# Another order of turns, key products, normalizations and layer borders in a two-layer attention kernel

## The chip, the cores and the metric

The kernel runs on one core of one Trainium2 chip. The metric is device time in microseconds (us) of one execution. All arithmetic is in 32-bit floating point.

## The reference

There are 8 sequences (batches) of 512 tokens with 512 features. A graph layer is followed by a self-attention layer with 16 heads. Cut to what matters:

```python
# layer 0: graph attention; every token attends to the first 20 tokens, in two directions d
self_feat = concat(x, cond) @ W_self.T + b_self
for d in range(2):
    aff = (self_feat @ Wq[d].T + bq[d]) . (self_feat[:, :20] @ Wk[d].T + bk[d])      # per head
    w = softmax(where(edges > 0, aff, NEG) + edge_bias)
    output += einsum(w, self_feat[:, :20]) @ Wout[d] + bout[d]
x = x + relu(output)
# layer 1: self-attention with conditional layer norm
h = gamma(cond) * layernorm(x) + beta(cond)
q, k, v = h @ Wqkv.T + bqkv
out = (softmax(q @ k.T) / sqrt(512)) @ v @ Wp.T + bp          # 16 heads of 32
h1 = out + x
return gamma * layernorm(h1) + beta + h1
```

## The kernel before, in words

Four engines compute: TensorE (PE) multiplies and transposes, VectorE (DVE), ScalarE (ACT) and GpSimd (POOL) do the rest; SyncE (SP) issues most transfers. Every engine works through its own queue in the order in which the program writes its instructions (`manual_schedule`), so the order of the lines in a step is the order on each engine. A tile pool with n buffers gives out its buffers in turn, and the next user waits until the last one's readers are through.

**Layer 0** walks 32 slots, one for each batch and each block of 128 tokens. For slot n it transposes the weights of slot n (`turn_weights`, tile `ptw`), normalizes those of slot n+1 (`normalize0`: exponential on ACT, sum and reciprocal on DVE, multiplication on POOL), and makes the scores of slot n+2 (`scores0`: `pss` on PE, an addition on DVE, then on POOL the mask L480 and the edge terms L481; `less_top`: maximum on DVE, subtraction on POOL). `result0` makes the slot's result (`po`), which DVE adds to x and SP writes to `mid`. In the last slots PE gets products of layer 1 for batch 0 between them: `q_or_k` and `value` (`pqk`, `pv`).

**Layer 1** walks 128 steps: 7 batches of 16 steps (4 head groups g times 4 token blocks c), and a last batch of 16 steps with the token blocks outermost. `at` is the step's number in its batch, 0 to 15. In step n:

- `scores(n+1)` (PE, tile `s`), `tops(n+1)` (DVE, two maxima over 1024 elements), `exps(n+1)` (ACT, four exponentials), `normalize(n+1)` (DVE `reciprocal` of `den`, then POOL multiplies each of four tiles `e`), in two pairs of heads;
- `turn_probs(n, j)`: PE transposes one of four `e` tiles into a PSUM bank `pt`, and ACT or DVE copies it to `et`;
- in even steps `weigh(n-2)` and `weigh(n-1)` (PE, tile `pao`), in the last batch one `weigh` in every step;
- two job slots (`job(b, 2*at)` and `job(b, 2*at+1)`), one ahead of the transposes of j = 2 and one ahead of those of j = 3. The list `JOBS[b]` fills them: products for the next batch's queries, keys and values (`product`, tile `pst`; seven products each, by a Strassen scheme whose sums of token quarters `token_sums` and of weights `weight_sums` are made ahead), or the output projection of the batch before (`project`, `ppj`). `None` is a hole. A product's bank is emptied by DVE (L715, L722, L724), a projection's too (L737).
- `turn(b+1, f)`: PE transposes 128 features of the next batch's normalized tokens Z into a bank `pz`, and ACT (L127) or DVE (L129) writes the gated result to HT. `norm_stats` and `norm` make Z.
- `finish(b, c, part)` for finished blocks: "statistics" on DVE and POOL, "norm" on DVE (L749, L750), "sums" on POOL (L753, L754) with the transfer to `out`. The table `FINISH` says in which step.

The banks `pt`, `pst`, `ppj`, `pz` come from one ring of three (`ps_g`), `pao` from a ring of one (`ps_a`): a transpose or product waits until the bank three users back has been emptied.

Of the kernel before, what the change touches and what calls it, by code (L numbers as in the profile page):

```python
# [19 lines left out]
P = 128  # L20
# [24 lines left out]
def graph_then_self_attention(ctx: ExitStack, tc: tile.TileContext, x, x_t, near, near_t, labels, w_self_t, wq, wk_t,  # L45
# [68 lines left out]

        nc.gpsimd.tensor_tensor(XQ[b][:, c, :], XQ[b][:, c, :], bp_bc, ALU.add)

    def turn(b, f, by_scalar=True):

        if f == 0:
            pool = turned if b == 1 else feat  # L120
            HT[b] = pool.tile([P, C, N], F32, tag="turned" if b == 1 else "feat", name=f"ht_{b}")
        pz = bank(f"pz_{b}_{f}")
        for c in range(C):
            nc.tensor.transpose(pz[:, c * P:(c + 1) * P], Z[b][:, c, f * P:(f + 1) * P], ident)  # L124
        factor, term = (gates_t[:, i, f, b:b + 1] for i in range(2))
        if by_scalar:
            nc.scalar.activation(HT[b][:, f, :], pz, AF.Identity, bias=term, scale=factor)  # L127
        else:
            nc.vector.tensor_scalar(HT[b][:, f, :], pz, factor, term, ALU.mult, ALU.add)  # L129

    class Group:

# [38 lines left out]
    with ExitStack() as l0:  # L171
# [295 lines left out]
        def scores0(b, c):  # L467
            cut = slice(c * P, (c + 1) * P)
            pss = pair(f"pss_{b}_{c}")
            for i in range(2):  # L470
                on = slice(i * HM // 2, (i + 1) * HM // 2)
                o = pss[:, i, :HM // 2]
                for k in range(C):
                    nc.tensor.matmul(o, SF[b][:, k, cut], KQ[b][:, k, on], start=(k == 0), stop=(k == C - 1))  # L474
            t = three.tile([P, H, D2], F32, tag="t", name=f"t_{b}_{c}")
            nh = H // 2
            for i in range(2):
                nc.vector.tensor_tensor(t[:, i * nh:(i + 1) * nh], pss[:, i, :HM // 2].rearrange("p (h e) -> p h e", h=nh),
                                        QR[b][:, i * HM // 2:(i + 1) * HM // 2].rearrange("p (h e) -> p h e", h=nh), ALU.add)
            nc.gpsimd.tensor_tensor(t, t, MASK[b][:, c, None].to_broadcast([P, H, D2]), ALU.mult)  # L480
            nc.gpsimd.tensor_tensor(t, t, ADD[b][:, c, None].to_broadcast([P, H, D2]), ALU.add)  # L481
            T[b, c] = t

        def less_top(b, c):
            t = T[b, c]
# [65 lines left out]

        slots = [(b, c) for b in range(B) for c in range(C)]
        scores0(*slots[0])
        less_top(*slots[0])
        scores0(*slots[1])
        normalize0(*slots[0])
        less_top(*slots[1])
        for c in (0, 1):
# [3 lines left out]
        load_vt(2)  # L562
        for n, (b, c) in enumerate(slots):
            turn_weights(b, c)
            if n + 1 < len(slots):
                normalize0(*slots[n + 1])
            if n + 2 < len(slots):
                scores0(*slots[n + 2])
            if b + 1 + c // 2 < B:
                self_feat(b + 1 + c // 2, ((c + 2) % 4,))  # L570
            if 26 <= n < len(slots) - 2:
# [7 lines left out]
            if n in (24, 25):  # L579
                for f in (2 * (n - 24), 2 * (n - 24) + 1):  # L580
                    turn(0, f)
            for i in {26: (0,), 27: (1,), 29: (2,), 30: (3,)}.get(n, ()):
                group = q_or_k(i, 0) if i < 2 else value(i - 2)
                group.half(0)
                group.half(1)
            if n == 10:
                gate_columns(gb)
            result0(b, c)
            if n < 26:
                less_top(*slots[n + 2])  # L590
            if b + 1 + c // 2 < B:
# [29 lines left out]
                norm_stats(0, n - 15, early)  # L621
            for i in {22: (0, 1), 23: (2, 3)}.get(n, ()):
                norm(0, i, early)
            if n == 30:
                for i in range(C):
                    norm_stats(1, i)
            if n == 31:
                for i in range(C):
                    norm(1, i)

# [176 lines left out]
    def normalize(n, pair):  # L809
        at = slice(2 * pair, 2 * pair + 2)  # L810
        nc.vector.reciprocal(DEN[n][:, at], DEN[n][:, at])  # L811
        for j in (2 * pair, 2 * pair + 1):
            nc.gpsimd.tensor_scalar(E[n][j], E[n][j], DEN[n][:, j:j + 1], att_scale, ALU.mult, ALU.mult)  # L813

    def turn_probs(n, j, copy):
        pt = bank(f"pt1_{n}_{j}")
# [5 lines left out]
    def weigh(n):  # L822
        b, g, c = steps[n]
        last = b == B - 1
        if c == 0 or last:
            PAO[b, g] = ps_a.tile([P, 512], F32, tag="pao", name=f"pao_{b}_{g}_{c}")
        at = slice(c * P, (c + 1) * P)
        for k in range(C):
            for j in range(4):
                h = 4 * g + j  # L830
                nc.tensor.matmul(PAO[b, g][DH * j:DH * (j + 1), at], V[b][:, k, DH * h:DH * (h + 1)],  # L831
                                 ET[n, j][:, k, :], start=(k == 0), stop=(k == C - 1))
# [19 lines left out]
    def made(i, *ns):  # L852
        return [("product", i, n) for n in ns]

    def out_of(*cs):
        return [("project", c, n) for c in cs for n in range(2)]

    q, k, v = 0, 1, 2
    keys_and_queries = (made(q, 1, 2, 6, 5) + made(k, 1, 2, 6) + made(q, 3) + made(k, 5, 3)
                        + made(q, 4, 7) + made(k, 4, 7))  # L860
    JOBS = {0: [("own", i, f, n) for i, f in ((k, 1), (q, 2), (k, 2), (q, 3), (k, 3)) for n in range(2)]
            + made(v, 1, 2, 6, 5, 3, 7, 4) + [None] + keys_and_queries}
    for b in range(1, B - 1):
        pp = out_of(0, 1, 2, 3)
        JOBS[b] = [("turn", 1), ("turn", 2)] + pp + made(v, 1, 2, 6, 5, 3, 7, 4) + [None] + keys_and_queries

    JOBS[B - 2][4:17] = [pp[2], None] + pp[3:] + made(v, 1, 2) + [None] + made(v, 6, 5, 3)
    LAST = made(v, 4, 7) + [("project", B - 2, 0, 0), None]
    for job in ((B - 2, 0, 1), (B - 2, 1, 0), (B - 2, 1, 1), (B - 2, 2, 0), (B - 2, 2, 1), (B - 1, 0, 0), (B - 1, 0, 1), (B - 2, 3, 0),
                (B - 1, 1, 0), (B - 1, 1, 1), (B - 2, 3, 1), (B - 1, 2, 0), (B - 1, 2, 1)):  # L870
        LAST += [("project",) + job, None]
    JOBS[B - 1] = LAST

    FINISH = {}
    for b in range(1, B):
        for block, first, second in (((b - 1, 0), 2, 4), ((b - 1, 1), 4, 6), ((b - 1, 2), 6, 8), ((b - 1, 3), 7, 9)) if b < B - 1 else (
                ((b - 1, 0), 2, 3), ((b - 1, 1), 4, 5), ((b - 1, 2), 6, 7), ((b, 0), 8, 9), ((b, 1), 11, 12), ((b - 1, 3), 12, 13),
                ((b, 2), 14, 15)):
            FINISH.setdefault((b, first), []).append(block + ("statistics",))
            for part in ("norm", "sums"):  # L880
                FINISH.setdefault((b, second), []).append(block + (part,))
    OWN = {}

    def finish_parts(part):
# [4 lines left out]
    def job(b, slot):  # L889
# [4 lines left out]
        if kind == "own":  # L894
            i, f, n = of
            if n == 0:
                OWN[0] = q_or_k(i, f)
            OWN[0].half(n)
        elif kind == "turn":
            turn(b + 1, of[0], by_scalar=False)  # L900
        elif kind == "product":
            product(b + 1 if b < B - 1 else b, *of)
        else:
            project(*(of if b == B - 1 else [b - 1] + of))

    with tc.manual_schedule():
# [5 lines left out]
        scores(0)  # L912
        for pair in range(2):
            tops(0, pair)
        for pair in range(2):
            exps(0, pair)
        for group in (value(2), value(3)):
            group.half(0)
            group.half(1)
        for pair in range(2):  # L920
            normalize(0, pair)
        group = q_or_k(0, 1)
# [3 lines left out]
        for n, (b, g, c) in enumerate(steps):  # L926
# [3 lines left out]
            if more:  # L930
                scores(n + 1)
                for pair in range(2):
                    tops(n + 1, pair)
            if b == 0 and at < 4:
                turn(1, at)
            elif at < 2 and not last:
                turn(b + 1, 3 * at)
            if last and at > 0:
                if at > 1:
                    weigh(n - 2)  # L940
# [6 lines left out]
            if b + 2 < B:  # L947
                for i in range(2) if at == 12 else ():
                    norm_stats(b + 2, i)
                for i in range(C) if at == 14 else ():  # L950
                    norm(b + 2, i)
            early = n % 2 == 0 or last
            if more and early:
                exps(n + 1, 0)
            turn_probs(n, 0, nc.scalar.copy)
            if more and last:
                exps(n + 1, 1)
            turn_probs(n, 1, nc.vector.tensor_copy if last else nc.scalar.copy)
            if more and not early:
                exps(n + 1, 0)  # L960
            if more and not last:
                exps(n + 1, 1)
            if n > 0 and n % 4 == 0 and (not last or at == 0):
                outputs(n - 1)
            job(b, 2 * at)
            if more:
                normalize(n + 1, 0)
            if last:
                finish_parts("norm")
            finish_parts("statistics")  # L970
            if at in (12, 13) and b + 2 < B:
                norm_stats(b + 2, at - 10)
            if b == 0 and at < 12:
                weight_sums((v, q, k)[at // 4], at % 4)
            turn_probs(n, 2, nc.vector.tensor_copy if 0 < b < B - 1 and at < 2 else nc.scalar.copy)
            job(b, 2 * at + 1)
            if more:
                normalize(n + 1, 1)
            turn_probs(n, 3, nc.vector.tensor_copy)

            finish_parts("sums")
            sums = at - (4 if b == 0 else 1)
            if 0 <= sums < 3 and b + 1 < B:
                for i in {0: (0,), 1: (1, 2), 2: (3,)}[sums]:
                    token_sums(b + 1, i)
            if at == 9 and b > 0 and b + 2 < B:
                fetch(b + 2)
            for i, when in enumerate(range(C) if last else (10, 11, 12, 15)):
                if at == when:
# [61 lines left out]
```

## Time and profile before

| | us |
|---|---|
| median of 3 runs | 1345.51 (1344.25 to 1348.13) |
| the profiled execution | 1345.76 |
| its span, first to last instruction | 1344.0 |
| PE busy | 1314.8 (98%) |
| DVE busy | 957.6 (71%) |
| POOL busy | 757.6 (56%) |
| ACT busy | 668.1 (50%) |

The profiled execution is 0.25 us above the median, and 1.76 us of it lie outside its span. Durations come from that one execution. Matmul rows overlap: a row starts while the one before it still drains, so that a step of PE is measured from the start of one `s` row to the start of the next.

### The profile page before, as it was taken

The page shows a single profiled execution, that of the slowest core. Times are in us where ns is not written, and L with a number is a line of the kernel's source. Part 1 is how long each engine was busy: PE and PEld are TensorE (multiplying, and loading weights), DVE is VectorE, ACT ScalarE, POOL GpSimd, SP SyncE. Part 2 cuts the span into 40 slices and gives each one's busy share as a digit, 9 for nine tenths or more (in the row PEclk, how much of TensorE's full clock was granted, in tenths as well). Part 3 has the DMA queues.
Part 4 walks back from the last instruction along what each step waited for, and adds up shares of the span by engine and source line. Part 5 has one row for each costly group of instructions (what it writes and reads, how often), then busy time and mean ns, then how long its engine had stood idle before and what let it go on. Part 6 is the DMA issues. An engine that isn't in the chain of part 4 may idle for free.

```text
span 1344.0 us, 29289 instructions
## 1 busy us (share of the span) xinstructions
PE 1314.8 (98%) x11251; PEld 969.2 (72%) x11251; DVE 957.6 (71%) x1746; ACT 668.1 (50%) x1639; POOL 757.6 (56%) x867
## 2 busy tenths in 40 slices
PE   9999999999999999999999999999999999999997
PEld 6566666666664677777777777777777777777775
DVE  4567777677644578677767868777786877776886
ACT  1322223222225656665656566565665656665664
POOL 0255654555652455566466556646655664764776
PEclk9999999999999999999999999999999999999999
DMA  9624452252221000001002000100200010010010
GB/s 333 199 85 143 146 189 88 94 182 100 90 79 55 2 2 1 2 17 64 2 9 71 2 2 17 64 2 10 71 2 1 25 57 1 17 33 1 10 41 32
DMA packets 46521, 78.63 MB, mean 59 GB/s; under 512 B 9872, under 2 KB 14416, under 8 KB 46384
## 3 DMA queue, kind: packets, MB, share of 16 engines
q1 hardware_dynamic: 45440, 75.57, 16.5%
q8 instruction: 90, 1.47, 0.4%
q0 software_dynamic: 512, 0.66, 0.2%
q10 hardware_dynamic: 432, 0.55, 0.1%
q14 instruction: 47, 0.39, 0.1%
HBM read 59.27 MB, written 17.49 MB: 57 GB/s over the span
## 4 chain that ended last, share of the span: by engine, by line
PE 87%; DVE 8%; POOL 2%; DMA 1%; issue 1%; ACT 1%; POOLq 0%; SPq 0%; DVEq 0%; ACTq 0%
PE pst L700 17%; PE pt L818 17%; PE s L794 10%; PE pao L831 9%; PE pss L474 8%; PE ppj L735 7%; PE psf L303 6%; PE pqk L141 2%; PE po L515 2%; DVE top L801 1%; PE pz L124 1%; DVE o L750 1%; PE pw L443 1%; PE ptw L503 1%; PE pq L424 1%
## 5 line engine op out<-in xcount | busy, mean ns | idle before, releaser
L813 POOL TENSOR_SCALAR e<-e,den 128x512 f32<-128x512 f32 x512 | 362.7, 708 | 356.6 <-DVE den L811 256.5
L806 ACT ACTIVATE e<-s,top 128x512 f32<-128x512 f32 x512 | 349.2, 700 | 169.2 <-DVE top L801 169.2
L801 DVE TENSOR_REDUCE top<-s 128x2 f32<-128x1024 f32 x256 | 301.1, 1217 | 27.1 <-PE s L794 26.5
L818 PEld LDWEIGHTS pt<-ident,e 128*128 128x128 f32 x2048 | 234.1, 141 | 95.2 <-issue 41.7
L818 PE MATMUL pt<-ident,e 128*128 128x128 f32 x2048 | 290.9, 276 | 10.6 <-DVE den L811 6.2
L820 ACT COPY et<-pt 128x512 f32<-128x512 f32 x356 | 200.1, 596 | 133.4 <-PE pt L818 132.3
L794 PE MATMUL s<-k_pair,q_pair 32*128 32x512 f32 x992 | 144.9, 640 | 0.0
L474 PE MATMUL pss<-kq,sf 128*128 128x320 f32 x512 | 143.2, 433 | 1.0 <-DVE kq L431 1.0
L831 PEld LDWEIGHTS pao<-et,v 128*32 128x32 f32 x4096 | 107.4, 110 | 49.3 <-issue 48.5
L831 PE MATMUL pao<-et,v 128*32 128x128 f32 x4096 | 126.7, 274 | 0.5 <-ACT ao L847 0.5
L474 PEld LDWEIGHTS pss<-kq,sf 128*128 128x128 f32 x512 | 94.9, 190 | 37.5 <-ACT sf L310 1.5
L735 PE MATMUL ppj<-w,ao 128*128 128x256 f32 x496 | 117.9, 381 | 0.0
L303 PE MATMUL psf<-vt,ws 128*128 128x512 f32 x256 | 115.0, 592 | 0.0
L806 ACT ACTIVATION_READ_ACCUMULATOR e<-s,top 128x1 f32 x512 | 110.0, 215 | 0.0
L820 DVE COPY et<-pt 128x512 f32<-128x512 f32 x156 | 105.4, 675 | 2.5 <-PE pt L818 2.4
L735 PEld LDWEIGHTS ppj<-w,ao 128*128 128x128 f32 x496 | 89.4, 190 | 11.0 <-ACT ht L127 1.4
L497 POOL TENSOR_TENSOR t<-t,den 128x640 f32<-128x640 f32 x32 | 40.8, 1274 | 83.5 <-DVE den L496 82.9
L303 PEld LDWEIGHTS psf<-vt,ws 128*128 128x128 f32 x256 | 48.3, 190 | 50.7 <-issue 46.6
L505 ACT COPY wt<-ptw 128x640 f32<-128x640 f32 x32 | 22.2, 693 | 106.8 <-PE ptw L503 106.4
L737 DVE TENSOR_TENSOR xq<-ppj,xq 128x256 f32<-128x256 f32 x62 | 26.3, 424 | 61.1 <-PE ppj L735 61.1
L492 ACT ACTIVATE t<-t 128x640 f32<-128x640 f32 x32 | 23.6, 737 | 80.1 <-POOL t L489 80.1
L489 POOL TENSOR_TENSOR t<-t,top 128x640 f32<-128x640 f32 x32 | 40.7, 1273 | 37.4 <-DVE top L488 37.4
(236 smaller groups left out, 1935.5 us busy)
## 6 DMA issues: line engine op xcount, KB each, us to landing
x<-in_x SPq DMA_DIRECT2D x8, 1024.0 KB
mid<-x SPq DMA_DIRECT2D x32, 256.0 KB
xq<-mid SPq DMA_DIRECT2D x8, 1024.0 KB
out<-o SPq DMA_DIRECT2D x31, 256.0 KB
vt<-in_x_t SPq DMA_DIRECT2D x7, 1024.0 KB
labels<-in_labels SPq DMA_DIRECT2D x16, 440.0 KB
wq<-in_wq SPq DMA_DIRECT2D x4, 1024.0 KB
gate<-gates SPq DMA_DIRECT2D x8, 512.0 KB
```

Of the source, the lines that this page charges most:

```text
L303: nc.tensor.matmul(psf[f], ws[:, k, f * P:(f + 1) * P], VT[b][:, k, :], start=(k == 0), stop=(k == C - 1))
L474: nc.tensor.matmul(o, SF[b][:, k, cut], KQ[b][:, k, on], start=(k == 0), stop=(k == C - 1))
L497: nc.gpsimd.tensor_tensor(tv, tv, den.to_broadcast([P, 2 * H, NG]), ALU.mult)
L700: nc.tensor.matmul(out[:, m, :], fixed[:, k, m * P:(m + 1) * P], moving[:, k, :], start=(k == 0), stop=(k == 1))
L735: nc.tensor.matmul(out, AO[b, k][:, c * P:(c + 1) * P], wp[:, k, on], start=(k == 0), stop=(k == C - 1))
L794: nc.tensor.matmul(S[n][j // 2][:, j % 2, :], Q[b, g][on, c * P:(c + 1) * P], K[b, g][on, :], start=True, stop=True)
L801: nc.vector.tensor_reduce(TOP[n][:, 2 * pair:2 * pair + 2], S[n][pair], AX.X, ALU.max, negate=True)
L806: nc.scalar.activation(e, S[n][pair][:, j % 2, :], AF.Exp, bias=TOP[n][:, j:j + 1], accum_out=DEN[n][:, j:j + 1])
L813: nc.gpsimd.tensor_scalar(E[n][j], E[n][j], DEN[n][:, j:j + 1], att_scale, ALU.mult, ALU.mult)
L818: nc.tensor.transpose(pt[:, k * P:(k + 1) * P], E[n][j][:, k * P:(k + 1) * P], ident)
L820: copy(et, pt.rearrange("p (k n) -> p k n", k=C))
L831: nc.tensor.matmul(PAO[b, g][DH * j:DH * (j + 1), at], V[b][:, k, DH * h:DH * (h + 1)], ET[n, j][:, k, :], start=(k == 0), stop=(k == C - 1))
```

## The change

It alters only orders, places and engines; every matmul of before is there after. In six parts:

1. **Turns.** `turn(b+1, f)` runs at the head of steps 1 to 4, one block of features in each, always with ACT. Before, blocks 0 and 3 were at the head of steps 0 and 1 and blocks 1 and 2 in the job slots of step 0, the latter two with DVE (for batch 1: all four at the heads of steps 0 to 3).
2. **Keys.** Key products 4 and 7 of a batch move from its predecessor's step 15 to its own step 0 ("late"). In the last batch it is the value products 4 and 7, in slots 0 and 2 (before: 0 and 1).
3. **Holes.** The two slots that this frees become holes in the second slots of steps 10 and 12, beside the one in step 8; the order of the query and key products changes with it.
4. **Finishing.** In batches 1 to 6 the "norm" parts stand in steps 4, 6, 6, 8 (before: 4, 6, 8, 9), the statistics in steps 2 to 5 (before: 2, 4, 6, 7). `token_sums` follow the turns by a step or so. The third block's copy in steps 0 and 1 goes from DVE to ACT. The next-but-one batch is fetched a step earlier.
5. **Between the layers.** In slot 29 the last slot's scores are summed on DVE ahead of slot 30's denominators, and its edge terms are added by DVE (`add_edges`) and not by POOL. `value(1)` and `value(2)` are put around the last two slots' transposes and results. Batch 1's `norm_stats` and `norm` move from layer 0's last slots behind layer 1's first `tops` and into its step 0.
6. **The end.** In the last batch the blocks are finished in order (6,0) to (6,3), (7,0) to (7,2), always at an odd step; step 1 takes the order of copies and exponentials that odd steps have in other batches; the last `weigh` gets a bank of the ring of three; the last step's `e` for j = 3 is scaled by DVE, and its second reciprocals stand behind the copy.

```diff
@@ layer 0
+        def add_edges(b, c, engine=nc.gpsimd):
+            engine.tensor_tensor(T[b, c], T[b, c], ADD[b][:, c, None].to_broadcast([P, H, D2]), ALU.add)
...
+            if n + 3 == len(slots):
+                scores0(*slots[n + 2])
             if n + 1 < len(slots):
                 normalize0(*slots[n + 1])
+            if n + 3 < len(slots):
+                scores0(*slots[n + 2])
             if n + 2 < len(slots):
-                scores0(*slots[n + 2])
+                add_edges(*slots[n + 2], nc.vector if n + 3 == len(slots) else nc.gpsimd)
...
-            for i in {26: (0,), 27: (1,), 29: (2,), 30: (3,)}.get(n, ()):
-                group = q_or_k(i, 0) if i < 2 else value(i - 2)
+            group = {26: lambda: q_or_k(0, 0), 27: lambda: q_or_k(1, 0), 29: lambda: value(0), 30: lambda: value(1),
+                     31: lambda: value(2)}.get(n, lambda: None)()
+            if group:
                 group.half(0)
-                group.half(1)
+                if n < 30:
+                    group.half(1)
...
             result0(b, c)
+            if n >= 30:
+                group.half(1)
@@ layer 1
-            nc.gpsimd.tensor_scalar(E[n][j], E[n][j], DEN[n][:, j:j + 1], att_scale, ALU.mult, ALU.mult)
+            engine = nc.vector if n + 1 == len(steps) and j == 3 else nc.gpsimd
+            engine.tensor_scalar(E[n][j], E[n][j], DEN[n][:, j:j + 1], att_scale, ALU.mult, ALU.mult)
...
-        if c == 0 or last:
+        if n + 1 == len(steps):
+            PAO[b, g] = bank(f"pao_{b}_{g}_{c}")
+        elif c == 0 or last:
...
+    late = [("late", k, n) for n in (4, 7)]
+    JOBS = {b: (late + out_of(0, 1, 2, 3) if b else own) + made(v, 1, 2, 6, 5, 3, 7, 4) + [None]
+            + made(q, 1, 2) + made(k, 1) + [None] + made(q, 6, 5) + made(k, 2) + [None] + made(k, 6) + made(q, 3) + made(k, 5, 3)
+            + made(q, 4, 7) + [None] for b in range(B - 1)}
+    JOBS[B - 2][14:] = (made(v, 3) + made(q, 1, 2) + [None] + made(q, 6, 5) + made(k, 1) + [None] + made(k, 2, 6) + made(q, 3) + [None]
+                        + made(k, 5, 3) + made(q, 4, 7) + made(k, 4, 7))
+    JOBS[B - 1] = [("late", v, 4), None, ("late", v, 7)]
...
-        for block, first, second in (((b - 1, 0), 2, 4), ((b - 1, 1), 4, 6), ((b - 1, 2), 6, 8), ((b - 1, 3), 7, 9)) if b < B - 1 else (
-                ((b - 1, 0), 2, 3), ((b - 1, 1), 4, 5), ((b - 1, 2), 6, 7), ((b, 0), 8, 9), ((b, 1), 11, 12), ((b - 1, 3), 12, 13),
+        for block, first, second in (((b - 1, 0), 2, 4), ((b - 1, 1), 3, 6), ((b - 1, 2), 4, 6), ((b - 1, 3), 5, 8)) if b < B - 1 else (
+                ((b - 1, 0), 2, 3), ((b - 1, 1), 4, 5), ((b - 1, 2), 6, 7), ((b - 1, 3), 8, 9), ((b, 0), 10, 11), ((b, 1), 12, 13),
                 ((b, 2), 14, 15)):
...
-        for group in (value(2), value(3)):
-            group.half(0)
-            group.half(1)
+            if pair == 0:
+                group = value(3)
+                group.half(0)
+                group.half(1)
...
-            if b == 0 and at < 4:
-                turn(1, at)
-            elif at < 2 and not last:
-                turn(b + 1, 3 * at)
+            if n == 0:
+                for i in range(C):
+                    norm(1, i)
+            if 0 < at <= C and not last:
+                turn(b + 1, at - 1)
...
-            early = n % 2 == 0 or last
+            each = last and at != 1
+            early = n % 2 == 0 or each
```

## The prediction

> **What bounds the kernel now.** I read the page first, then the chain at the border of the layers, then the rows of each engine in order of time. On the page:
>
> ```profile
> PE 1314.8 (98%) x11251; PEld 969.2 (72%) x11251; DVE 957.6 (71%) x1746; ACT 668.1 (50%) x1639; POOL 757.6 (56%) x867
> PE 87%; DVE 8%; POOL 2%; DMA 1%; issue 1%; ACT 1%; POOLq 0%; SPq 0%; DVEq 0%; ACTq 0%
> ```
>
> PE is the bound, and the change leaves its work alone. It can only win back what PE loses in small waits, 13% of the chain at most. There are three places. The first is the border of the layers, in the chain in order of time (start, us, what):
>
> ```profile
> 391.74 1.55 POOL t L480
> ...
> 393.36 1.55 POOL t L481
> ...
> 399.26 1.28 POOL t L497
> ...
> 400.58 0.78 PE ptw L503 x5
> ...
> 404.74 1.22 DVE top L801
> ...
> 406.77 8.80 PE pv L141 x16
> ```
>
> From 391.7 to 400.6 one slot's mask, edges, maximum, subtraction, exponential, sum and scaling run in a row while PE ends its other work at 398.7; from 404.6 to 406.8 PE waits for DVE to empty a bank. And 16 `pv` matmuls take 8.80 us where 16 at the usual 0.43 take 6.9. The stretches say why (PE, PEld, DVE, ACT, POOL busy, then PE's granted clock):
>
> ```profile
> 407.00:411.00 4.00, 4.00 (x6) 1.58 (x6) 2.65 (x6) 1.83 (x6) 1.15 (x2) 0.57 0.27 96
> 411.00:415.00 4.00, 4.00 (x11) 1.73 (x10) 0.17 (x1) 0.65 (x2) 1.64 (x3) 1.00 0.92 363
> ```
>
> The clock was halved behind the idle time: the wait costs twice, first as itself and then as five `pv` at 0.85 in place of 0.43.
>
> The second place is step 9 of every batch, here batch 2. DVE's rows, then PE's:
>
> ```profile
> 598.28 0.54 DVE L749 TENSOR_SCALAR o<-xq,mv_h 128x512 f32<-128x512 f32 x1
> 598.85 0.69 DVE L750 TENSOR_TENSOR o<-o,gate 128x512 f32<-128x512 f32 x1
> ...
> 604.51 1.33 DVE L749 TENSOR_SCALAR o<-xq,mv_h 128x512 f32<-128x512 f32 x1
> 605.87 1.65 DVE L750 TENSOR_TENSOR o<-o,gate 128x512 f32<-128x512 f32 x1
> 607.44 0.68 DVE L715 TENSOR_TENSOR q_pair<-pst,vec 128x512 f32<-128x512 f32 x1
> ```
>
> ```profile
> 601.06 1.21 PE L794 MATMUL s<-k_pair,q_pair 32*128 32x512 f32 x8
> ...
> 605.34 1.89 PE L700 MATMUL pst<-ht,w 128*128 128x256 f32 x8
> 608.27 0.63 PE L818 MATMUL pt<-ident,e 128*128 128x128 f32 x4 [1.03 <-DVE den L811]
> 608.82 1.14 PE L794 MATMUL s<-k_pair,q_pair 32*128 32x512 f32 x8
> ```
>
> A step of PE is 1.07 for `s`, 1.02 for the first two `pt` (0.44 each and 0.15 for the switch), 1.73 for each product, 0.44 for each later `pt`: 6.43 odd, 8.31 even with `pao` (1.88). Step 9 lasts 608.82 - 601.06 = 7.76, so 1.33 are lost: DVE's norm takes 2.98 instead of 1.23 beside POOL's sums, the bank of the product is emptied at 608.12, and the last `pt` needs that bank.
>
> The third is the last batch, where a wait of ACT's copies holds PE:
>
> ```profile
> PE pt L818 <- ACT et L820: 2.9, 5, 1.1
> ```
>
> **The change part by part.** (a) *Border, part 5.* PE's own work from the last `pss` (ends 388.17) to `s_1` is four `pv` (4 x 3.43), `pqk` 3.43, three `po` (1.55), two `ptw` (0.55), `s` 1.07 = 24.0 with switches 24.2, so `s_1` could start at 412.3; it starts at 418.94. 6.6 are lost. After: DVE adds at 388.4 (before at 390.28, behind `den`), mask 389.3 to 390.9. The edge terms go to DVE: no such row; the nearest is L750 with two SBUF inputs, 0.69 for 512 elements; L495's sum over 640 takes 0.82, which I take. It meets POOL's L497 (1.27), now behind the mask. The row: L750 takes 1.65 for its 0.69 beside POOL's L754, and 1.06 beside POOL's scalings L813, at 1259.1. [...] Free of it the addition ends at 391.8[...]. The rest of the chain is as before, 5.6 (394.93 to 400.53): `t` is ready at 397.4 or 398.6. PE, with half of `value(1)` and `value(2)` on either side, reaches that `ptw` at 398.7; cost nothing either way, 0.1 to 1.3 of margin. `po_7_3`, the rest of `value(2)`, `s_0` at 404.3 follow with no wait; DVE empties the last `po` at 403.4, and `pv` 3 needs only ACT's copy, 405.1. Four statistics (3.95 in a row before) now stand on DVE behind both maxima and ahead of the reciprocals, with POOL's four powers (0.55) ahead of `e_0`: first `e_0` at 413.4, PE wants it at 413.3; `pt` loses 0.2 to 0.4. The norms (1.91) behind `tops(1)` delay `e_1` to 418.7, wanted at 420. Gain 6.3, bounds 3 and 6.8.
>
> (b) *Turns and keys, parts 1 and 2.* Before: steps 0 and 1 of batch 2 last 543.01 - 536.39 = 6.62 and 550.27 - 543.01 = 7.26; their content is 6.31 and 6.87; 0.7 are lost, 0.26 of it as the projection at 545.74 waits for ACT to empty the `pz` bank (ring of three). After, steps 1 and 3 have that same order (`s`, `pz`, two `pt`, projection): 2 x 0.26. In even steps `pao` covers ACT's 0.78, but `pz` behind `s` and `pao` behind `pz` pay the 0.15 switch once more (net one more per batch). Paid: 0.7. So nothing is won. ACT has 4.3 in a step with three copies of 0.53, and 5.1 with a turn, of 6.9: hidden; DVE is freed of 1.6. Late k4 and k7 put 2.0 of L724 into step 0, an 8.3 step in which DVE has 3.3 else: hidden; keys of pair 1 are used in step 7. Behind the late v7 waits step 114's `pao`, 3 us later.
>
> (c) *Finishing, part 4.* The norm leaves step 9: 1.33 back in batches 1 to 6. Two norms in step 6: DVE before had `tops` to 583.2, one norm to 584.5 and then 1.11 of waiting for the product at 585.4. A second norm (1.26) ends at 585.7: 0.2 late, and the bank is due at 587.4. But POOL, with t2 and t3 in step 4 (1.28 each), runs about 2.3 late into step 6, and its t4 (two inputs) meets a norm. [...] By the rows 0.37 + 0.9, PE loses 0 to 0.5; I take 0.3. POOL's four sums there (5.2) leave e_40 0.35 of margin. Fetch on SP: one step earlier and still behind the same `out` issue, read four steps later; nothing. In the last batch the gate's transfer falls behind one `out` issue, two steps ahead of its use as before; nothing.
>
> (d) *Holes, part 3.* PE only gives the 1.73 to step 0. The hole of step 8 ran without loss (`e_41` at 601.15, `pt` at 602.20). In step 12 DVE has `tops` 2.36, three statistics 3.0, k2 0.87, reciprocals 0.3, copy 0.67 = 7.2 for 6.58 of PE: reciprocal at 6.6 into the step, second scaled `e` at 8.4, wanted at 8.3. 0.2 lost, 0 to 0.6. Batch 0 has weight sums before its holes; there one `pt` lost 0.35 in step 9, and it will again after step 10: 0.4 more.
>
> Batches 1 to 5: 2.03 won, 0.7 + 0.3 + 0.2 paid = 0.8 each, 4.1. Batch 6, without statistics: 1.1. Batch 0: -0.4. Middle: 4.8.
>
> (e) *The end, part 6.* Step 1 lasts 1247.12 - 1241.22 = 5.90 with content 4.69: `pt` waits for ACT's copy behind two exponentials. With odd order and the moved v7 this goes: 1.2. Step 12 lasts 1320.61 - 1313.38 = 7.23, as norm and statistics share it; the steps after a norm alone last 6.22, the others 5.8 to 5.95. After: 0.8 won. From 1326.91 to 1334.04 PE does 4.9 of work in 7.13: POOL brings `e` 2 and 3 of the last step at 1329.9 and 1330.8, and `pao` waits 0.49 for the ring of one. POOL without a sum in step 12 is 0.5 earlier, one `e` (0.7 to 0.8) is DVE's (by L749, 0.54, up to 1.06), the bank wait goes: 1.6. DVE's last norm then stands behind the last copy, idle until the last projection. End: 3.6, bounds 1.5 and 5.
>
> Sum: 6.3 + 4.8 + 3.6 = 14.7, all inside the span; what lies around it, and the 6.3 us from the last matmul to the end, stay. 1345.76 - 14.7 = 1331.1, less 0.25, by which the profiled execution stands above the median: **1330.8**. [...]
>
> **The rivals.** *The border pays half* (15%): POOL's place in the queue, or the bank for `pv` 3, holds PE another 3 us[...]. For: several semaphores gate it and the margins are 0.1 to 0.3. Against: PE has products to run. 1335.5. *The stall only moves* (17%): step 6 or 12 loses another 1.0 in six batches, for which the 1.33 of step 9 speaks; against, POOL stood idle for 4.6 at that norm. 1336.8. *Slower* (4%): the doubled norm in step 6 collides in full, 2 x 2.98. DVE then has 10.7 for 8.31 of PE (2.4 lost), POOL's sums start late and hold `e_40` (1.3), and steps 8 and 12 lag 1.0: 5.4 a batch instead of 1.2, 6 x 4.2 = 25: 1356. It decides from 4.4 a batch on; POOL's other rows in step 6 are scalings, which cost 0.37. *Nothing arrives* (4%): half of border and end and no middle, 1341 to 1346. *Better* (8%): step 6 and 12 lose nothing and border and end come in full: 1326.
>
> **How the numbers follow.** The main case (52%) spans 1328 to 1334. A measurement of this kernel tells 0.3% or 4 us from no change. 8 in 10 reach from 1326.5 over border and moved stall to 1338. Faster by more than 4 us (below 1341.5) are the main case, better, the half border and the moved stall but for 1% of its tail: 0.91; same are that 1% and "nothing arrives": 0.05; slower 0.04.
>
> **What would show it.** Right: `ptw` without a wait for POOL near 398.7, no half clock at the border, `s_1` near 412.5; step 9 at 6.43; projections of steps 1 and 3 still 0.26 late; the last batch's step 1 near 6.5 without a wait for `et`. Wrong: a wait of `pt` in steps 6, 7 or 12 above 0.6, L749 and L750 of step 6 above 2 us together per block, or a batch period (116.64 now) that falls by less than 0.4 or by over 1.5.

## The result

| | us |
|---|---|
| before, median of 4 runs | 1344.88 (1344.19 to 1348.13) |
| changed, median of 4 runs | 1335.14 (1334.97 to 1335.69) |
| ratio, 95% interval | 0.9924 (0.9906 to 0.9941) |
| the changed kernel's profiled execution, its span | 1335.18, 1333.4 |

The changed kernel is faster by 9.7 us. Forecast were 14.7, from 1345.51 to 1330.8, in a range of 1326.5 to 1338.0: the sign and the range held, and a third of the gain did not come.

The page of the changed kernel, the rows that answer to those of before (engines, then the chain that ended last):

```profile
PE 1314.7 (99%) x11251; PEld 967.4 (73%) x11251; DVE 943.7 (71%) x1723; ACT 683.2 (51%) x1664; POOL 755.6 (57%) x865
PE 86%; DVE 8%; POOL 2%; issue 2%; DMA 1%; ACT 1%; POOLq 0%; SPq 0%; DVEq 0%; ACTq 0%
```

PE's busy time is the same to 0.1 us, but that is the sum of two opposite changes: between the last `pss` and the end of `s_1` it falls from 27.5 to 25.3, and in each of batches 1 to 5 it rises by 0.37. The chain's shares hardly move; they do not tell where time was won. What tells is the length of each step, from the end of its `s` row to the end of the next. Worked out from PE's rows, batch 2 (counted from 0, as everywhere below):

```
step             0    1    2    3    4    5    6    7    8    9   10   11   12   13   14   15 | batch
before        6.75 7.12 8.31 6.43 8.31 6.42 8.31 6.43 6.64 7.70 8.31 6.43 8.31 6.43 8.31 6.43 | 116.64
changed       8.31 7.13 8.89 7.12 8.90 6.43 8.53 6.43 6.64 6.48 6.58 6.54 6.58 6.73 8.52 6.43 | 116.23
recip_first   8.31 7.13 8.90 7.12 8.90 6.43 8.53 6.43 6.64 6.43 6.58 6.43 6.58 6.43 8.52 6.43 | 115.76
keys_first    8.31 7.13 8.90 7.12 8.90 6.43 8.53 6.43 6.64 6.47 6.58 6.53 6.58 6.73 8.31 6.43 | 116.01
old_middle    6.75 7.12 8.31 6.43 8.31 6.43 8.31 6.43 6.65 6.47 8.31 6.43 8.31 6.43 8.31 6.43 | 115.41
orders_odd    8.31 6.99 8.90 6.99 8.90 6.43 8.31 6.43 6.64 6.43 6.58 6.43 6.58 6.43 8.31 6.43 | 115.06
```

(The rows below the second are experiments.) Steps 10 and 12 are shorter by the 1.73 of the product that left them. Step 9 won 1.22. But steps 6, 11, 13 and 14 each became longer with no work added.

The fronts of two executions differ (the last `pss` ended at 388.33 before and at 388.73 after), so the sum is made from there to the last matmul: 949.43 before, 938.42 after, 11.0 won. By parts, with the two products (3.46) that move from batch 0 to batch 6 set against each other: border to `s_1` +6.48, batch 0 -1.56, batches 1 to 5 +0.41 each, batch 6 +0.55, the last batch +3.49. These are profiled executions: the one of before stands 0.88 above the median of the table, and the front of the changed one is 0.40 longer, so that 11.0 here are 9.7 there.

**The border.** The chain in order of time (start, us, what), then a stretch of the windows view (PE, PEld, DVE, ACT, POOL busy, PE's granted clock, DMA share, GB/s):

```profile
399.25 0.55 PE ptw L503 x5
399.80 1.72 PE pv L138 x4
...
404.79 1.07 PE s L799 x8
405.86 3.63 PE pv L138 x8
409.49 3.43 PE pqk L138 x8
412.93 1.08 PE s L799 x8
```

```profile
407.00:411.00 4.00, 4.00 (x10) 1.71 (x9) 3.83 (x10) 2.86 (x8) 1.11 (x2) 1.00 0.99 346
```

The chain goes through PE alone where it went through POOL, DVE and ACT; eight `pv` take 3.63 where 16 took 8.80 (0.45 for 0.55 each); the clock is 1.00 where it was 0.57. Of the 6.48, 4.26 are PE's idle time, which is gone, and 2.21 are busy time; some 1.7 of the latter (an estimate) are the half of the 3.41 us that the granted clock stood at 0.50 (shown below).

**The end.** PE's waits for ACT's copies were 2.9 us in five, all in the last batch. The waits for POOL's `e`, there too, were these (what waits, for what, us in total, times, longest):

```profile
PE pt L818 <- POOL e L813: 1.1, 2, 0.8
```

In the changed kernel the same two waits are

```profile
PE pt L824 <- ACT et L826: 1.6, 6, 0.4
PE pt L824 <- POOL e L819: 0.8, 1, 0.8
```

One of the six, 0.37, is in step 0 of batch 0, so 1.2 are left in the last batch. The second line, at 1319.7, is the tail's wait for one `e`: it became shorter and did not go.

### The profile page after: what moved, and what is told of

The parts are those of the page before. It is cut to its first block, busy times and chain, and to the rows that moved or that the text cites. A ratio compares the mean times of both kernels' runs of the same rounds, so it can differ in the third digit from the quotient of the medians.

```text
span 1333.4 us, 29328 instructions
## 1 busy us (share of the span) xinstructions
PE 1314.7 (99%) x11251; PEld 967.4 (73%) x11251; DVE 943.7 (71%) x1723; ACT 683.2 (51%) x1664; POOL 755.6 (57%) x865
## 4 chain that ended last, share of the span: by engine, by line
PE 86%; DVE 8%; POOL 2%; issue 2%; DMA 1%; ACT 1%; POOLq 0%; SPq 0%; DVEq 0%; ACTq 0%
PE pst L705 18%; PE pt L824 16%; PE s L799 9%; PE pss L471 9%; PE pao L839 8%; PE ppj L740 8%; PE psf L300 6%; PE po L515 2%; PE pqk L138 2%; DVE top L806 2%; PE pz L124 1%; PE ptw L503 1%; PE pw L440 1%; PE pq L421 1%; PE pv L138 1%
## 5 line engine op out<-in xcount | busy, mean ns | idle before, releaser
L826 ACT COPY et<-pt 128x512 f32<-128x512 f32 x369 | 208.8, 595 | 105.1 <-PE pt L824 103.9
L826 DVE COPY et<-pt 128x512 f32<-128x512 f32 x143 | 96.7, 677 | 3.1 <-PE pt L824 2.8
L126 ACT ACTIVATE ht<-pz,gates_t 128x512 f32<-128x512 f32 x32 | 24.7, 778 | 74.2 <-PE pz L124 74.2
```

Of the source, the lines that this page charges most:

```text
L826: copy(et, pt.rearrange("p (k n) -> p k n", k=C))
```

## The experiments

Each is the changed kernel with one edit. Times are medians.

### border_back and edges_pool: the border

```diff
# border_back: part 5 undone
# edges_pool
-                add_edges(*slots[n + 2], nc.vector if n + 3 == len(slots) else nc.gpsimd)
+                add_edges(*slots[n + 2])
```

> The changed kernel with part 5 undone (the border between the layers as before, batch 1's statistics and norms back in the last slots). Theory: in the changed kernel s_1 comes 6.08 us sooner, but 0.58 of that is given back in step 0, where PE waits for e_0, e_1 and a copy. So undone it is 1335.1 + 5.5 = 1340.6 us (1339.5 to 1341.6), with the idle DVE, the wait of ptw for POOL and pv at half clock back. Rival: the give-back in batch 0 (1.56 in all) belongs to the border's statistics and norms: then only +4.5, 1339.6, and the waits of steps 11, 13, 14 of batch 0 are gone. Rival: step 0 loses the same either way: +6.1, 1341.2.

> The changed kernel; only the last slot's edge terms are added by POOL as in the other slots. DVE's addition took 1.88 us in the changed kernel (391.37 to 393.25), beside POOL's L497 (391.30 to 392.57); alone some 0.82 was estimated. POOL's additions take 1.53, and this one would stand behind L497: from 392.6 to 394.1, 0.9 later, so that the last scaling ends at 399.8, and PE reaches ptw at 399.25: some 0.5 lost, 1335.6 us (1335.2 to 1336). Rival: PE has other work behind it and nothing is lost: 1335.1. Rival: the short wait makes more of itself (clock, bank of pv): 1337.

border_back: 1341.0 us (1339.72 to 1343.81), 5.9 above the changed kernel, so the border is worth nearly what was forecast of it (6.3), and batch 0 kept its waits: steps 11, 13 and 14 at 6.90, 6.73 and 8.52. Those do not belong to the border (first rival out). Step 0 stays at 7.22 as well, though no statistics and norms stand there: PE does not wait for `e` in it, and waits longer for ACT's copy of j = 0. So the border gives nothing back in step 0, and the second rival is the one that came (1341.2; the medians alone, with this spread, would not tell it from 1340.6).

The spread of 4.1 us is news. The profile fell on the slowest execution, and there the clock is halved twice. First four stretches of before, then of border_back, cut where the granted clock changes and in steps of the same length (same columns as above: the length, PE's busy time, and behind the engines the clock):

```profile
397.10:400.52 3.42, 1.76 (x15) 1.52 (x13) 2.51 (x6) 1.21 (x2) 1.27 (x2) 1.00 0.21 80
400.52:403.94 3.42, 2.96 (x23) 2.47 (x27) 2.87 (x12) 0.69 (x1) 1.67 (x4) 1.00 0.47 150
403.94:407.35 3.41, 1.27 (x10) 0.37 (x3) 2.61 (x5) 1.35 (x4) 0.55 (x1) 1.00 0.00 0
407.35:410.76 3.41, 3.41 (x6) 1.35 (x5) 2.30 (x5) 1.25 (x5) 0.91 (x2) 0.50 0.29 103
```

```profile
399.72:403.13 3.41, 1.27 (x11) 1.02 (x10) 3.27 (x10) 0.69 (x1) 2.32 (x3) 1.00 0.46 112
403.13:406.55 3.42, 3.42 (x18) 2.66 (x18) 1.22 (x8) 0.00 (x0) 0.61 (x2) 0.50 0.18 42
406.55:409.96 3.41, 1.26 (x10) 0.47 (x3) 2.71 (x5) 1.45 (x4) 0.55 (x1) 1.00 0.00 0
409.96:413.37 3.41, 3.41 (x5) 1.36 (x5) 2.20 (x5) 1.24 (x4) 1.01 (x2) 0.50 0.41 120
```

PE has the same three waits in both: 1.73 for `ptw`, 0.40 for `po`, and 2.13 or 2.15 for the bank of `pv`. Each of these three stretches at half clock lasts 3.41 us and follows one of 3.41 in which PE was busy for 1.27 or 1.26; behind 1.76 and 2.96 the clock stayed. In before the first two waits lie in two different stretches, in border_back in one. In all thirteen traces a stretch between two records of the granted clock is a whole multiple of 3.413 us (118, 1 and 273 times that in before; 388 times in the changed kernel; 115, 1, 1, 1 and 271 times in border_back), and the first record lies 4.4 to 10.6 us behind the start of the span. What decides whether the clock falls is not shown beyond these stretches.

The times follow. Of border_back's 13 executions the fastest has a mean clock of 1.000, the four slowest 0.996. Both kernels with the old border scattered (before from 1343.7 to 1348.8 over all its executions); every one with the new border stayed within 1.6 us.

edges_pool: 1335.82 us (1335.39 to 1336.29), 0.7 slower, as expected. The rows of the edge terms and of the `ptw` behind them, first of the changed kernel, then of edges_pool:

```profile
391.30 1.27 POOL L497 TENSOR_TENSOR t<-t,den 128x640 f32<-128x640 f32 x1
391.37 1.88 DVE L481 TENSOR_TENSOR t<-t,add 128x640 f32<-128x640 f32 x1 [0.60 <-POOL t L477]
399.09 0.71 PE L503 MATMUL ptw<-ident,t 128*128 128x128 f32 x5
```

```profile
391.65 1.27 POOL L497 TENSOR_TENSOR t<-t,den 128x640 f32<-128x640 f32 x1
392.88 1.54 POOL L481 TENSOR_TENSOR t<-t,add 128x640 f32<-128x640 f32 x1
400.11 0.77 PE L503 MATMUL ptw<-ident,t 128*128 128x128 f32 x5 [0.50 <-POOL t L497]
```

DVE's addition began 0.07 behind POOL's scaling and lasted 1.88, where the prediction took 0.82: 1.20 until POOL was through, then 0.68. POOL's took 1.27, which is also the mean of its 32 scalings. The prediction had the addition end at 391.8, with nothing lost beside POOL; it ended at 393.25. No row shows this addition alone, so that it is not shown how much of the 1.88 was waiting. It cost nothing, since PE came to `ptw` no sooner; on POOL it ended later still, and PE waited 0.50.

### norms_back: the table of part 4

```diff
-        ... ((b - 1, 0), 2, 4), ((b - 1, 1), 3, 6), ((b - 1, 2), 4, 6), ((b - 1, 3), 5, 8) ...
+        ... ((b - 1, 0), 2, 4), ((b - 1, 1), 4, 6), ((b - 1, 2), 6, 8), ((b - 1, 3), 7, 9) ...
-            if at == 8 and b > 0 and b + 2 < B:
+            if at == 9 and b > 0 and b + 2 < B:
```

> The changed kernel with the old table of statistics (steps 2, 4, 6, 7) and norms (4, 6, 8, 9) and the fetch in step 9. Theory: step 9 is back at 7.70 (+1.22), step 6 at 8.31 (-0.22): +1.0 in each of six batches, 1341.1 us (1340 to 1342). Rival: step 9's loss came from what stood around it before (keys, copies of DVE) and not from the norm: +0 to 2, 1335 to 1337, with step 9 below 7. Rival: the old loss returns and step 6 keeps its 0.22, which then is not the norm's: 1342.4.

1341.32 us (1340.34 to 1341.73). In each of batches 1 to 6 step 6 is at 8.31 and step 9 at 7.70 (batch 6: 7.94): all but 0.05 of step 9's wait (batch 6: 0.29) was the norm's, and the 0.22 of step 6 are the price of two norms there. Moving the norms is worth 6.2 us.

Where the 0.22 come from, the changed kernel's DVE and POOL in step 6 of batch 1 (batches are numbered from 0; the prediction's rows "of batch 2" are this one's):

```profile
580.19 1.50 DVE L754 TENSOR_SCALAR o<-xq,mv_h 128x512 f32<-128x512 f32 x1
581.72 0.69 DVE L755 TENSOR_TENSOR o<-o,gate 128x512 f32<-128x512 f32 x1
582.33 0.68 DVE L729 TENSOR_TENSOR v<-pst,v 128x512 f32<-128x512 f32 x1
```

```profile
579.81 1.59 POOL L690 TENSOR_TENSOR t<-ht,t 128x512 f32<-128x512 f32 x1
```

The second norm runs into POOL's last token sum and takes 2.19 in place of 1.23; the product's bank behind it is emptied at 583.0, and the transpose that wants it begins 0.2 late.

### recip_first and keys_first: the holes of part 3

In a step with a hole, here step 12 of batch 1, DVE's rows, then POOL's and PE's rows of the `e` and `pt` that follow:

```profile
620.83 0.69 DVE L93 BATCH_NORM_STATS2 st<-xq 128x6 f32<-128x512 f32 x1
621.55 0.18 DVE L95 BATCH_NORM_AGGREGATE mv<-st 128x2 f32<-128x6 f32 x1
621.77 0.15 DVE L96 TENSOR_SCALAR mv<-mv 128x1 f32<-128x1 f32 x1
622.20 0.88 DVE L727 SCALAR_TENSOR_TENSOR k_pair<-pst,b_less,k_pair 128x256 f32<-128x256 f32 x2 [0.27 <-PE pst L705]
622.99 0.15 DVE L816 RECIPROCAL den<-den 128x2 f32<-128x2 f32 x1
```

```profile
623.24 1.47 POOL L819 TENSOR_SCALAR e<-e,den 128x512 f32<-128x512 f32 x2 [0.69 <-DVE den L816]
624.03 1.40 PE L824 MATMUL pt<-ident,e 128*128 128x128 f32 x8
```

DVE is idle for 0.27 ahead of L727, waiting for the product; its queue holds the reciprocal behind that, though the `den` that it needs were written by ACT before 620.4. The two `e` are then ready at 623.9 and 624.7, and the first two `pt` of step 13 take 1.40 in place of 1.09. In a full step the second product gives 1.73 of cover; a hole takes the cover away. The first edit only swaps these two in the queue; the second puts another product into the last slot of step 14.

```diff
# recip_first
+            ahead = not last and at in (8, 10, 12)
+            if ahead:
+                normalize(n + 1, 0)
             job(b, 2 * at)
-            if more:
+            if more and not ahead:
                 normalize(n + 1, 0)
# keys_first
-            + made(q, 1, 2) + ... + made(k, 6) + made(q, 3) + made(k, 5, 3)
+            + made(q, 1, 2) + ... + made(k, 6, 5, 3) + made(q, 3)
```

> The changed kernel; only in steps 8, 10 and 12 of batches 0 to 6 the reciprocal of the first pair (and POOL's scalings behind it) stands ahead of the job, so that on DVE it is not behind the emptying of that product's bank. No work is moved to another step. Theory (order): where the second slot is a hole, that emptying ends 0.3 to 0.9 before the next step's pt wants its e, and the reciprocal stands behind it. Steps 9, 11 and 13 then lose nothing: 0.06 + 0.11 + 0.30 in batches 1 to 6, some 0.8 in batch 0: -3.5 us, 1331.6 (1331 to 1332.6). Rival (load, as the prediction had it): DVE has 7.2 us of work in step 12, so that the order is all the same: 1335.1, or later by what the bank then waits.

> The changed kernel; only key product 3 of a batch stands in the first slot of step 14 (behind key product 5), and query product 3 in the second (batches 0 to 5). Theory: step 14 lasts 8.52 in place of 8.31 since s of the next batch waits for DVE to add key product 3 into the keys, made in the last slot before it; query product 3 makes only tokens 256 to 511, which are wanted two steps later. -0.21 in six batches: -1.27, 1333.9 us (1333.5 to 1334.3), step 14 at 8.31. Rival: s waits for its own bank, or for the queries as well: 1335.1, step 14 stays at 8.52.

recip_first: 1330.55 us (1330.28 to 1330.97), 4.6 below the changed kernel where 3.5 were expected: batch 0 gave 1.2 and not 0.8, and batch 6, which loses 0.29 in step 9, 0.7. Steps 9, 11 and 13 are at 6.43 in every batch, in batch 0 too (there 6.84, 6.90 and 6.73 in the changed kernel). DVE has the same work in step 12 as ever:

```profile
619.69 0.15 DVE L96 TENSOR_SCALAR mv<-mv 128x1 f32<-128x1 f32 x1
619.76 0.15 DVE L816 RECIPROCAL den<-den 128x2 f32<-128x2 f32 x1
620.11 0.88 DVE L727 SCALAR_TENSOR_TENSOR k_pair<-pst,b_less,k_pair 128x256 f32<-128x256 f32 x2 [0.20 <-PE pst L705]
```

```profile
620.56 1.47 POOL L819 TENSOR_SCALAR e<-e,den 128x512 f32<-128x512 f32 x2
621.95 1.09 PE L824 MATMUL pt<-ident,e 128*128 128x128 f32 x8
```

The reciprocal stands in the time in which DVE was idle. So it was order, and not load: the prediction's sum for this step (7.2 of DVE's work for 6.58 of PE) counted the right instructions and drew the wrong bound from them.

keys_first: 1334.11 us (1333.78 to 1334.55), step 14 at 8.31 in batches 0 to 5. The end of step 14 in the changed kernel, then in keys_first:

```profile
637.47 0.60 PE L824 MATMUL pt<-ident,e 128*128 128x128 f32 x4
637.67 0.88 DVE L727 SCALAR_TENSOR_TENSOR k_pair<-pst,b_less,k_pair 128x256 f32<-128x256 f32 x2 [1.41 <-PE pst L705]
638.22 1.14 PE L799 MATMUL s<-k_pair,q_pair 32*128 32x512 f32 x8
```

```profile
637.82 0.60 PE L824 MATMUL pt<-ident,e 128*128 128x128 f32 x4
638.35 1.14 PE L799 MATMUL s<-k_pair,q_pair 32*128 32x512 f32 x8
```

`s` follows its `pt` by 0.75, without the keys in between by 0.53 (there the two rows overlap by 0.07). In the changed kernel it could have begun at 638.0; it begins at 638.22, as the first of the two additions of key product 3, which makes its keys, has ended (638.16). The query product in its place makes only later tokens.

### old_middle: parts 1 to 3 undone

```diff
-    JOBS = {b: (late + out_of(0, 1, 2, 3) if b else own) + ... }
+    (the lists of before for batches 0 to 6)
-            if 0 < at <= C and not last:
-                turn(b + 1, at - 1)
+            if b == 0 and 0 < at <= C:
+                turn(1, at - 1)
+            elif b > 0 and at < 2 and not last:
+                turn(b + 1, 3 * at)
-    SUMS_AT = {..., False: {2: (0,), 4: (1, 2), 5: (3,)}}
+    SUMS_AT = {..., False: {1: (0,), 2: (1, 2), 3: (3,)}}
```

> The changed kernel with parts 1 to 3 undone for batches 1 to 6 (turns 0 and 3 at the heads of steps 0 and 1, 1 and 2 in job slots with DVE, key products 4 and 7 in step 15, one hole in step 8, the old order of products, token sums in steps 1 to 3, in batch 0 the old list behind the own products); the table of norms, the border and the end stay as changed. Theory (the ledger of the traces): parts 1 to 3 win nothing in steps 0 to 4 and cost 0.67 in steps 9, 11, 13 and 14 of a batch, some 1.0 in batch 0; and without the late token sum the two norms of step 6 cost nothing: -6 us, 1329 us (1328 to 1331.5), steps 6, 9, 11, 13 and 14 at 8.31, 6.43, 6.43, 6.43, 8.31. Rival: the new places of turns and token sums are what makes room for the new norms: step 4 or 6 then loses 0.5 to 1.5 a batch, 1332 to 1338.

With parts 1 to 3 go back the old token sums and the third block's copy with DVE, which stand under part 4; in batch 0 only the list of jobs is the old one.

1329.52 us (1329.27 to 1329.93): the changed kernel is 5.6 us faster with these taken out of it. By the steps: 0.98 in batch 0, 0.82 in each of batches 1 to 5 (116.23 to 115.41), 0.55 in batch 6, 5.6 in all. Nothing else moved, and the new norms need neither the new turns nor the late token sums: step 6 is at 8.31 here.

### end_back: part 6 undone

```diff
# the last batch's jobs, finishing table, order of copies, banks and engines as before, for example
-            each = last and at != 1
+            each = last
```

> The changed kernel with part 6 undone (last batch as before, with its two value products in step 0). Theory: -3.5 is the end's part by the traces (1.35 in step 1, 0.96 in steps 12 and 13, 1.18 behind the last s): 1338.6 us (1338 to 1339.3). Rival: the last batch's step 1 was late because of what batch 6 left it, which is changed too: 1337.3, step 1 at its content.

1338.26 us (1337.62 to 1339.18): +3.1 by the medians, +3.4 by the traces from the last `pss` on. It is lost in the last batch alone: 1.35 in steps 0 and 1 together, 0.96 in steps 12 and 13 (5.90 and 7.28 in place of 6.43 and 5.79), the rest behind the last `s`. So the last batch's step 1 was late by its own order (rival out).

### turns_behind, all_orders, orders_odd, old_middle_orders: other orders

```diff
# turns_behind: the turn of steps 1 to 4 behind the transposes of j = 1
-            if 0 < at <= C and not last:
-                turn(b + 1, at - 1)
             ...
             turn_probs(n, 1, nc.vector.tensor_copy if each else nc.scalar.copy)
+            if 0 < at <= C and not last:
+                turn(b + 1, at - 1)
# all_orders: turns_behind, recip_first, keys_first, and
+            early = (n % 2 == 0 and n > 0) or each
+            engine = nc.vector if n + 1 == len(steps) and j > 1 else nc.gpsimd
+            (the second norm of step 6 behind normalize(n + 1, 0))
# orders_odd: all_orders, with the turns of steps 2 and 4 at the head again
# old_middle_orders: old_middle with what of all_orders applies to it
```

> The changed kernel; only the turn of steps 1 to 4 stands behind the transposes of j = 1 instead of at the head of the step (PE, and the copy on ACT). Theory: in steps 1 and 3 the job takes the bank of pz, which ACT has just begun to empty (0.26 each), and in all four the switch behind s is paid once more (0.15 in even steps, where pao follows). Then the ring gives the job the bank of j = 0 and ACT's turn fits into its wait for the maxima: steps 1 and 3 at 6.87 in place of 7.13, steps 2 and 4 at 8.75 in place of 8.90: -0.82 in seven batches, -5.5 us, 1329.6 (1329 to 1331). Rival: the turn now stands ahead of the exponentials on ACT and the e of the next step come late: steps 2 to 5 lose as much as is won, 1335 or more. Rival: the 0.26 come from the projection's own inputs: only the switches go, 1333.4.

> The changed kernel with all orders that the traces point to: reciprocal ahead of the job in steps 8, 10, 12; key product 3 ahead of query product 3; turns behind the transposes of j = 1; in step 0 of batch 0 the copies ahead of the exponentials; the second norm of step 6 behind the reciprocal instead of ahead of the product's emptying; both late e of the last step scaled by DVE. Theory: the parts add up: -4.6 (measured), -1.1 (measured), -5.5, -0.5, -1.3 (0.22 in six batches), -0.8 at the end: 1321.3 us (1320 to 1323). Rival: waits take each other's place: 1325 or more, with a new loss in steps 5, 7 or 9.

turns_behind: 1334.96 us (1334.62 to 1335.19), no gain, so the theory of it fell. Steps 1 and 3 win 0.13 instead of 0.26, and steps 2 and 4 lose 0.1 (0.25 once) where 0.15 were to be won. In an even step (ACT, then PE):

```profile
546.75 0.68 ACT L811 ACTIVATE e<-s,top 128x512 f32<-128x512 f32 x1
547.32 0.20 ACT L811 ACTIVATION_READ_ACCUMULATOR e<-s,top 128x1 f32 x1
547.56 1.07 ACT L826 COPY et<-pt 128x512 f32<-128x512 f32 x2
```

```profile
547.46 0.60 PE L124 MATMUL pz<-ident,z 128*128 128x128 f32 x4
548.20 1.99 PE L740 MATMUL ppj<-w,ao 128*128 128x256 f32 x8
```

The job now takes the bank of j = 0 instead of that of `pz`. ACT copies that out from 547.56, behind two exponentials, and the job begins as the copy ends. The wait changed its bank and its size. In odd steps the copies stand ahead of the exponentials; why 0.13 remain there is open.

all_orders: 1326.21 us (1325.94 to 1326.51), 4.9 above what was expected. The turns account for that: 5.5 were expected of them and none came. The other edits add up: steps 6, 9, 11, 13 and 14 at their content (the sum of PE's work in them), step 0 of batch 0 at 6.66 in place of 7.21, and 1.0 less behind the last `s`.

> As all_orders, but the turns of steps 2 and 4 stand at the head of the step again; those of steps 1 and 3 stay behind the transposes of j = 1. Theory: behind them the job takes the bank of j = 0, which ACT empties in an even step only behind two exponentials (9.00 and once 9.15 in place of 8.90), in an odd step ahead of them (6.99 in place of 7.13). So steps 2 and 4 return to 8.90: -0.1 in fourteen steps and -0.15 once, 1324.7 us (1324.2 to 1325.3). Rival: the even steps' 0.1 come from what the odd step before leaves: 1326.2.

> As old_middle (parts 1 to 3 undone), with the orders that still apply: reciprocal ahead of the job in step 8, the turns of step 1 (in batch 0 of steps 1 and 3) behind the transposes of j = 1, copies ahead of exponentials in step 0 of batch 0, both late e of the last step on DVE. Theory: 1329.5 less 0.7 (step 9), 1.0 (turns), 0.55 (step 0) and 1.0 (end): 1326.3 us (1325.7 to 1327). Against orders_odd it has nothing more to win: if the holes of part 3 cost only through the order behind them, orders_odd is at least as fast (by 0.16 a batch). Rival: the two late holes leave something that no order takes back: then this one is the fastest.

orders_odd: 1324.61 us (1324.15 to 1325.58), ratio to before 0.9838 (0.9825 to 0.9852); steps 2 and 4 are back at 8.90, which shows the place of their turn as the cause; that it acts through the exponentials ahead of the copy is read from the rows above. old_middle_orders: 1326.08 us (1325.56 to 1326.14). So the two ways of the middle end 1.5 us apart by the medians and 1.1 by the traces, in the other order than without the edits: with the reciprocal and the keys in place, the holes of part 3 cost nothing, and the changed middle is ahead by 0.16 a batch (115.06 to 115.22), which it wins in steps 0 to 4. orders_odd is the fastest kernel of this study, 10.5 us below the changed one. Its chain:

```profile
PE 92%; DVE 5%; POOL 1%; issue 1%; ACT 1%; DMA 0%; POOLq 0%; DVEq 0%; ACTq 0%
```

## Why the prediction was right, and where it was not

- **(a) border, 6.3 forecast:** 6.48 measured to `s_1`. The granted clock was 1.00 where it had been 0.57, `ptw` came at 399.1 without a wait. DVE's addition was taken at 0.82 and took 1.88; the margin named beside it (0.1 to 1.3) was what saved the sum, and 0.2 of it was left (the last scaling ended at 398.88). Step 0 lost 0.25 for `e`, as said (0.2 to 0.4), and another 0.56 that was not foreseen: a `pt` waits for ACT's copy of j = 0 behind two exponentials, which in that step wait for the maxima. The 0.25 cost nothing by themselves, as border_back shows: without them the copy holds PE for the whole 0.81. Step 0 has one turn less than before, which step 4 has instead, and is as long as before (7.21 for 7.22). One reading was off: the last `pss` ended at 388.33 and not at 388.17, so that 6.4 were to be won and not 6.6.
- **(b) turns and keys, 0 forecast:** steps 0 to 4 grew by 3.43 for 3.46 of work. Right, also in its 0.26 in steps 1 and 3 and in the 0.15 that it puts down to the switch (step 4: 8.31, 0.44 for `pz` and 0.15 are the 8.90 measured).
- **(c) finishing, +1.33 and -0.3 a batch:** +1.22 and -0.22. Right (from end to end of the `s` rows step 9 had only 1.27 to give, as the `s` ahead of it had begun some 0.06 early); the second norm's rows sum to 2.19, above the 2 named as a sign, and the cost is the one named.
- **(d) holes, -0.2 a batch:** this is the step that failed. Steps 9, 11, 13 and 14 of batches 1 to 5 lose 0.05, 0.11, 0.30 and 0.21, 0.67 in all. Of these, 0.30 was priced (0.2) but laid to DVE's load in step 12, which recip_first refutes. Step 11 was put at nothing, for the hole of step 8 had seemed to cost nothing; behind the norm's wait it did cost 0.05 in step 9, and does so without parts 1 to 3 too (6.47 in old_middle). And 0.21 were not seen at all: the sum followed the late key products forward and did not ask what the new order of the others puts into the last slot before `s`. In batch 0 the holes took 0.98 for 0.4. With the 0.58 of the turn that left step 0 counted in, the middle brought 1.05 in place of 4.8. That is the whole of what the traces lack (11.0 for 14.7).
- **(e) the end, 3.6 forecast:** 3.49 (1.35, 0.96 and 1.18 for 1.2, 0.8 and 1.6). The tail's missing 0.4 is POOL: the power of the last statistics stands ahead of `e` 2 (0.60 from 1319.08 on), and all_orders takes 1.0 back by giving that `e` to DVE.
- **The rivals.** "The stall only moves" came half true: it priced another 1.0 in each of six batches, and 0.47 more than forecast went (0.67 for 0.2), but in steps 11, 13 and 14, for which it had no place. The half border and the full collision in step 6 did not come. The batch period fell by 0.41, at the edge of the signs named (0.4 to 1.5). The time itself, 1335.1, lies outside the main case (1328 to 1334) and beside the figure of the half border (1335.5), whose cause did not come: that the range held is owed to border and end, and to its width.

With old_middle between the two, the 11.0 of the aligned traces fall apart by cause: the border 6.48; less 0.58, since batch 1's turn moved from step 0 to step 4 and step 0 did not become shorter; part 4's norms in the old middle 7.25 (1.23 in each of batches 1 to 5, from 116.64 to 115.41, and 1.1 in batch 6); the end 3.49; less 5.6 for parts 1 to 3, of which 1.3 is the collision in step 6 and the rest the order in the queues.

## What to carry to other kernels

A hole in an engine's work shortens the step for all who work beside it: before making one, list for each queue what stands ahead of the value that the next step wants first, and ask whether that can be ready, not whether the engine has the time. When the order of products changes, ask of each which consumer reads it first, and leave a slot between. And price a queue by order: of two instructions whose inputs come at different times, the one with the later input, if it stands first, holds both (the reciprocal of step 12 began at 622.99 behind the addition that waited for its product, and at 619.76 ahead of it).

## What was not expected of the hardware

- With the old border the executions of one kernel took between 4.6 and 8.7 us more than the changed kernel (border_back's 1339.72 and 1343.81 against 1335.14). In the profiled executions PE's idle times there were followed by one or by two stretches of 3.41 us at a granted clock of 0.50, each behind 3.41 us in which PE was busy for 1.27 or 1.26, though no single wait lasted over 2.15; with the new border every kernel's executions lay within 1.6 us.
- DVE's addition took 1.88 us, where 0.82 was taken, beside a POOL instruction that had begun 0.07 sooner, and POOL's took its usual 1.27.
